# Early loads and sums in an autocorrelation stage, stored operand sums, product order and the engine of a bias add

## The chip, the core and the metric

The kernel runs on one core of a Trainium2 chip. A core has a tensor engine (PE) for matrix products, VectorE (DVE), ScalarE (ACT) and GpSimd (POOL) for elementwise work, and SyncE (SP), whose queue issues the DMA transfers here. Each engine works through its own instructions in order. The metric is the device time of one execution in microseconds (us); several runs are given by their median. The kernel before takes 3541.73 us, the median of 3 runs (3533.64 to 3542.67).

## What is computed

The input `x` has 8 batches of 256 rows and 1024 columns, `ctx` likewise. Four blocks follow each other, each added to `x` with a gate, each on a layer norm of `x`:

```python
x = x + tanh(g_xattn[0]) * autocorrelation(norm(x), ctx, ctx)        # 8 heads, top 11 lags
x = x + tanh(g_ffn[0])   * lora_ffn(norm(x), W, b, A, B, gate_w, gate_b)
x = x + tanh(g_xattn[1]) * attention(norm(x), ctx, ctx, mask, wq, wk, wv, wo)
x = x + tanh(g_ffn[1])   * fourier_ffn(norm(x), W_base, b_base, enc0, enc1, coefs0, coefs1, ...)
...
# autocorrelation
qf, kf = fft(q, axis=2), fft(k, axis=2)
corr = ifft(qf * conj(kf), axis=2).real
w, idx = top_k(corr, 11); w = softmax(w)
out = sum_i w_i * v[min(idx_i + pos, L - 1)]
...
# fourier_ffn: base = x @ W_base.T + b_base; update = irfft of a low-rank product, scaled by 0.5
```

Attention has 32 query heads and 8 key and value heads of 128 columns, with rotary positions. All is in float32.

## The kernel before, in words

The batches go through in two passes (the loop at L1075) of four batches: eight tiles `xt` of 128 rows and 1024 columns stay in SBUF for the whole pass. A pass runs four stages one after the other: autocorrelation with the keys and values of attention beside it, `lora_ffn`, `attention`, `fourier_ffn`.

**Products by sevens.** Every large matrix product is cut into 2 x 2 blocks and done with seven block products instead of eight (Strassen's scheme in Winograd's form). Four of the seven operands of each side are sums: `left_operands` (L175) and `right_operands` (L184) make them with four instructions each. The products run in the order of the tuple `SEVEN` (L37), and `combine` (L192) or `add_product` (L224) spreads each over the result's quadrants:

```python
SEVEN = (1, 2, 6, 7, 5, 3, 4)
```

In `combine`, product 2 finishes quadrant (0,0), 5 finishes (1,1), 3 finishes (0,1) and 4 finishes (1,0). For 5, ACT copies the product and POOL adds it to `u` and to `w`; 3 then needs that `u`. In `add_product`, 7 makes `w` on DVE, and POOL adds it to two parts of `x` (L238, L239); 5 and 4 then add to those parts.

**Autocorrelation.** The Fourier transforms are matrix products with constant cosine and sine matrices. `turn` (L407) works on a half batch: one batch and 512 of its 1024 columns, so eight turns a pass and one more to end. It loads `cn`, `end` and `xr` (the context's two halves, one row of it, and the reversed second half of `x`), normalizes the two parts of `x` on ACT (`xn`, L424), and makes sums and differences on POOL: `ke`, `ko` from the context, `qe`, `qo` from `xn` (L428 to L431). `dft` (L377) transforms these; `products` (L391) multiplies spectra on DVE and adds on POOL (`re`, `im`); `correlation` transforms back, and `lags` (L520) finds the eleven largest lags on DVE and their softmax weights `w`. The sums of those, `both` (L505, L506), are the input of the second half of the work, which is done for the half batch `before` in the next turn: transposes (L468), spectra, products, and back with L483. Between these steps `fill(n)` takes the next pieces of `keys_values` (L653): the products for keys `ps_k` and values `ps_v` (L726), whose weights' sums are in pass 0 made on POOL (L142, L146), after the first weight's. The tile framework may place an instruction of one engine earlier or later than the text has it; the order in the engine's queue is then fixed.

SBUF tiles of 4 KB per partition come from rings of seven buffers, one for each group "a", "b" and "xn" (`big_tile`, L100). `xn`, the product tiles `ma` and `mb`, `w` and `both` share the group "xn".

**The last layer's weight.** `fold_last_layer` (L248), at the end of pass 0's autocorrelation, adds the low-rank Fourier update to `W_base`, so that the last feed-forward is one product. For each of eight tiles of 128 rows it loads a part of the weight (`w1in`, L283), two matmuls with 40 rows make the update (`acc`, L286; two PSUM buffers), DVE adds it (L293), and the sum is stored in DRAM as `w1_d` (L294).

**The feed-forwards.** Both work by pairs of row tiles. `ffn_weight` (L164) loads the four quadrants of the weight (eight loads of 512 KB by the class `Halves`) and returns a function that makes the four sums on DVE: eight instructions of 128x1024 at L128 (class `Both`). `lora_ffn` (L551) and `fourier_ffn` (L1016) call it in each pass, after the first pair's left operands. A pair is normalized (`xn`, L312), transposed on PE (L322), its left operands `s` are made (L178 to L181; on DVE for the first pair, on POOL after it), and seven products (L612 and L1053) are added to `x`. `fourier_ffn` adds its bias to each row tile on POOL in `prepare` (L1037). `lora_ffn` also multiplies by `ag` (L568), chooses a rank by DVE instructions, and multiplies by `bl`.

**Attention.** Sixteen steps a pass (two blocks of 512 rows, eight groups of heads). A step's queries are made in the step before (`ps_q`, L851; rotary in `rope`, L642, whose last add is on POOL, L651), `scores` (L891) is softmax of one batch n and one pair of heads, `values` (L928) applies the weights, and `outputs` (L864) multiplies with `wo` in the step after. In the first block of pass 0 the weights' sums are made on DVE and stored; later steps load all seven operands. `load_wq` and `load_wo` issue these loads on SP.

Of the kernel before, what the change touches and what calls it, by code (L numbers as in the profile page):

```python
# [18 lines left out]
P = 128  # L19
# [17 lines left out]
SEVEN = (1, 2, 6, 7, 5, 3, 4)  # L37
# [7 lines left out]
def flamingo_kernel(ctx: ExitStack, tc: tile.TileContext, a: dict, out: bass.AP):  # L45
# [39 lines left out]
    w1_d = dram.tile([2, 2, P, KH, HALF], F32, name="w1_d")  # L85
# [17 lines left out]
    class Halves:  # L103
# [5 lines left out]
        def load(self, src):  # L109
            for i, t in enumerate(self.t):  # L110
                nc.sync.dma_start(t, src[:, i * KQ : (i + 1) * KQ, :])

# [51 lines left out]
    def ffn_weight(eng, groups, src):  # L164
# [8 lines left out]
        return lambda: right_operands(Both(eng), q, t1, t2, t4)  # L173
# [74 lines left out]
    def fold_last_layer(group, pools):  # L248
# [32 lines left out]
        for c in range(KC):  # L281
            wt = big_tile(group, [2, HALF], "w1in")
            nc.sync.dma_start(wt, a["w1"][c * P : (c + 1) * P, :])  # L283
            for h in range(2):
                acc = ps_kv.tile([P, HALF], F32, tag="kv", name="acc")
                nc.tensor.matmul(  # L286
                    acc,
                    encr[:, c * P : (c + 1) * P],
                    dec[:, h * HALF : (h + 1) * HALF],
                    start=True,  # L290
                    stop=True,
                )
                nc.vector.tensor_add(wt[:, h, :], wt[:, h, :], acc)  # L293
            nc.sync.dma_start(w1_d[c // KH, :, :, c % KH, :].rearrange("h p d -> p h d"), wt)  # L294
            yield
# [39 lines left out]
    def autocorrelation(p, xt, pools, beside):  # L335
# [68 lines left out]

        def turn(this, before):  # L407

            if this:
                b, h = this  # L410
                cols = slice(h * HALF, (h + 1) * HALF)
                r0 = (p * BP + b) * S
                cn = w1.tile([P, 2, HALF], F32, tag="cn", name="cn")
                nc.sync.dma_start(
                    cn, a["ctx"][r0 : r0 + S, cols].rearrange("(s p) d -> p s d", p=P)
                )

                end = w1.tile([P, HALF], F32, tag="end", name="end")
                nc.sync.dma_start(end, a["ctx"][r0 + P, cols].partition_broadcast(P))
                xr = w1.tile([P, HALF], F32, tag="xr", name="xr")  # L420
                nc.sync.dma_start(xr, a["xr"][r0 // 2 : r0 // 2 + P, cols])
                xn = big_tile("xn", [2, HALF], "xn")
# [120 lines left out]
        for b in range(BP):  # L543
            for h in range(2):
                before = turn((b, h), before)
                if b == 0 and h == 0:
                    normalize(1, BP)
# [696 lines left out]
```

## Time and profile before

| what | value |
|---|---|
| median of 3 runs | 3541.73 us (3533.64 to 3542.67) |
| the profiled execution | 3532.26 us, its span 3530.3 us |
| PE busy | 3402.2 us, 96% of the span |
| DVE, POOL, ACT busy | 2203.3, 1460.3, 860.9 us |
| mean granted clock of PE | 0.980 |
| DMA | 418.86 MB, mean 119 GB/s |

The span runs from the first to the last instruction of the profiled execution. A busy share is that of all stages together. In the waits view a line names the instruction that waited and what released it, with the total, the number and the longest of these waits. In a timeline a line gives start, length, engine, source line, operation, output and inputs with shapes, how many of these in a row, and in brackets the engine's idle time before it with what ended it. The granted clock is the share of full speed that PE was given.

The stages of pass 0 lie, by the timeline, at about 0 to 422 us (autocorrelation, keys and values), 422 to 608 (the fold and the first feed-forward), 608 to 1681 (attention) and 1681 to 1799 (second feed-forward); those of pass 1 follow in the same way, up to 3530.

### The profile page before, as it was taken

How to read it: one execution, taken by the hardware profiler on the slowest of the kernel's cores; microseconds unless marked ns; L12 is line 12 of the kernel's file. 1: busy time of each engine (PE TensorE's matmuls, PEld its weight loads, DVE VectorE, ACT ScalarE, POOL GpSimd, SP SyncE). 2: the span in 40 equal slices, each digit the busy share in tenths (PEclk: the TensorE clock that was granted, in tenths of full speed). 3: DMA queues.
4: the chain of work that ended last, by engine and by line, in shares of the span. 5: the costliest groups of instructions: out<-in, count | busy, mean ns of one | idle time of the engine just before them, and what ended most of it. 6: DMA issues, size and time to landing. Idle time of an engine off the chain costs nothing. (4 is left out here: it accounts for less than half of the span.)

```text
span 3530.3 us, 37030 instructions
## 1 busy us (share of the span) xinstructions
PE 3402.2 (96%) x12888; PEld 2310.2 (65%) x12888; DVE 2203.3 (62%) x4141; ACT 860.9 (24%) x2065; POOL 1460.3 (41%) x1275
## 2 busy tenths in 40 slices
PE   7899999899999999999899999999999999999999
PEld 5666645776776776765456666567776776776644
DVE  7667456777777665666557575456566666566662
ACT  2222101222222322222122321113232322222220
POOL 4654212344443344345645542223344344344454
PEclk9999989999999999999999999999999999999999
DMA  6342523334333333333153433043333333333311
GB/s 231 128 151 92 178 98 109 124 132 146 128 133 127 117 123 124 117 125 102 48 200 104 147 99 126 1 155 100 124 117 123 114 122 121 121 116 123 113 39 48
DMA packets 158759, 418.86 MB, mean 119 GB/s; under 512 B 21060, under 2 KB 56132, under 8 KB 158574
## 3 DMA queue, kind: packets, MB, share of 16 engines
q1 hardware_dynamic: 158574, 416.51, 35.3%
q8 instruction: 102, 1.67, 0.2%
q14 instruction: 83, 0.68, 0.1%
HBM read 345.15 MB, written 71.30 MB: 118 GB/s over the span
## 5 line engine op out<-in xcount | busy, mean ns | idle before, releaser
L651 POOL TENSOR_TENSOR qT<-rope,rope 128x512 f32<-128x512 f32 x128 | 167.0, 1305 | 794.3 <-DVE rope L650 794.3
L880 PE MATMUL po<-wo,oT 128*128 128x512 f32 x960 | 432.4, 593 | 0.0
L851 PE MATMUL ps_q<-xn,wq 128*128 128x256 f32 x1920 | 431.5, 380 | 0.0
L851 PEld LDWEIGHTS ps_q<-xn,wq 128*128 128x128 f32 x1920 | 366.6, 191 | 51.3 <-PE po L621 0.5
L327 DVE SCALAR_TENSOR_TENSOR x<-po,tg,x 128x512 f32<-128x512 f32 x360 | 258.5, 742 | 196.9 <-POOL x L230 51.9
L913 ACT ACTIVATE s<-s,nmx 128x256 f32<-128x256 f32 x512 | 255.9, 500 | 299.0 <-DVE nmx L910 298.8
L908 DVE COPY_PREDICATED s<-keep,ps_s 128x512 f32<-128x512 uint8 x256 | 185.7, 728 | 220.4 <-PE ps_s L899 220.0
L880 PE MATMUL po<-wo,oS 128*128 128x512 f32 x640 | 287.4, 596 | 4.4 <-DVE c L220 4.4
L880 PEld LDWEIGHTS po<-wo,oT 128*128 128x128 f32 x960 | 175.8, 190 | 175.6 <-issue 165.2
L851 PE MATMUL ps_q<-xn_t,wq 128*128 128x256 f32 x1280 | 289.3, 379 | 0.0
L940 ACT COPY wT<-pt 128x512 f32<-128x512 f32 x256 | 137.9, 588 | 602.9 <-PE pt L934 602.9
L851 PEld LDWEIGHTS ps_q<-xn_t,wq 128*128 128x128 f32 x1280 | 243.2, 190 | 33.1
L899 PE MATMUL ps_s<-kT,qT 128*128 128x256 f32 x1024 | 251.0, 382 | 11.5 <-POOL qT L651 11.5
L945 PE MATMUL av<-wT,v 128*128 128x256 f32 x1024 | 246.0, 383 | 3.1 <-ACT wT L940 3.1
L945 PEld LDWEIGHTS av<-wT,v 128*128 128x128 f32 x1024 | 191.4, 190 | 77.8 <-issue 43.5
L648 DVE TENSOR_TENSOR rope<-c,tab 128x512 f32<-128x512 f32 x160 | 124.8, 780 | 162.5 <-POOL c L212 139.6
L922 DVE TENSOR_SCALAR s<-s,tot 128x256 f32<-128x256 f32 x512 | 220.4, 471 | 6.7
L907 POOL MEMSET s<- 128x512 f32 x256 | 129.4, 530 | 223.2 <-PE pt L934 221.6
L899 PEld LDWEIGHTS ps_s<-kT,qT 128*128 128x128 f32 x1024 | 192.3, 191 | 38.9 <-POOL qT L651 13.1
L880 PEld LDWEIGHTS po<-wo,oS 128*128 128x128 f32 x640 | 121.4, 191 | 146.0 <-issue 133.5
L910 DVE TENSOR_REDUCE nmx<-s 128x2 f32<-128x512 f32 x256 | 175.0, 685 | 8.3
L235 POOL TENSOR_TENSOR x<-x,part 128x512 f32<-128x512 f32 x80 | 105.0, 1314 | 152.6 <-DVE part L327 143.5
(260 smaller groups left out, 5755.3 us busy)
## 6 DMA issues: line engine op xcount, KB each, us to landing
wq<-in_wq_dram SPq DMA_DIRECT2D x104, 512.0 KB, 3.3
wo<-in_wo_dram SPq DMA_DIRECT2D x104, 512.0 KB, 3.3
wq<-wq_d SPq DMA_DIRECT2D x96, 512.0 KB, 3.3
wo<-wo_d SPq DMA_DIRECT2D x96, 512.0 KB, 3.3
wk<-in_wk_dram SPq DMA_DIRECT2D x26, 512.0 KB, 4.7
wv<-in_wv_dram SPq DMA_DIRECT2D x26, 512.0 KB, 3.9
wk<-wk_d SPq DMA_DIRECT2D x24, 512.0 KB, 4.3
wv<-wv_d SPq DMA_DIRECT2D x24, 512.0 KB, 3.3
```

Source lines behind the costliest of these rows:

```text
L327: nc.vector.scalar_tensor_tensor(xs, ps, g, xs, ALU.mult, ALU.add)
L651: nc.gpsimd.tensor_add(dst, t0, t1)
L851: nc.tensor.matmul(ps[:, l, :], wops[r][:, l, c, :], xo[r][:, c, :], start=(c == 0), stop=(c == KH - 1),)
L880: nc.tensor.matmul(po, ops[r][:, h, t * P : (t + 1) * P], wops[r][:, h, :], start=(h == 0), stop=(h == 1),)
L899: nc.tensor.matmul(ps[:, t, :], qT[i, n][:, l, t * P : (t + 1) * P], kT[:, n * S : (n + 1) * S], start=True, stop=True,)
L907: nc.gpsimd.memset(s, MASKED)
L908: nc.vector.copy_predicated(s, keep[b], ps)
L910: nc.vector.tensor_reduce(nmx, s, AX.X, ALU.max, negate=True)
L913: nc.scalar.activation(s[:, t, :], s[:, t, :], AF.Exp, bias=nmx[:, t : t + 1], accum_out=tot[:, t : t + 1],)
L922: nc.vector.tensor_scalar(s[:, t, :], s[:, t, :], tot[:, t : t + 1], None, ALU.mult)
L940: nc.scalar.copy(wT[i], pt)
L945: nc.tensor.matmul(av[:, i, :], kv[step][1][:, n * 2 + c, :], wT[i][:, c, :], start=(c == 0), stop=(c == 1),)
```

## The change

Four things change.

1. In autocorrelation, `turn` is cut up. `loads` issues the three loads of a half batch, `sums` does its normalization and its sums. A turn issues the loads of the next half batch at its start and makes its sums after the second `fill(2)`, ahead of the work for the half batch before. `end` has two buffers for that. `left` and `took`, the scratch tiles of `lags`, go from two buffers to one.
2. The feed-forward weights' sums are made once. `lora_ffn`'s are stored in DRAM in pass 0 (`w0_d`) and loaded in pass 1. `fold_last_layer` now works in four rounds on two row tiles each, makes the four sums of the last layer there on DVE and stores all seven operands (`w1_d`); `fourier_ffn` loads them in both passes (`stored_weight`: fourteen loads of 512 KB).
3. The order of the seven products is 1, 2, 6, 7, 4, 5, 3, everywhere; loads of stored operands follow it.
4. `fourier_ffn` adds its bias on DVE, at the start of a pair's `project`, instead of on POOL in `prepare`.

```diff
-SEVEN = (1, 2, 6, 7, 5, 3, 4)
+SEVEN = (1, 2, 6, 7, 4, 5, 3)
+WEIGHTS = (1, 2, 3, 5, 6, 4, 7)
...
-    w1_d = dram.tile([2, 2, P, KH, HALF], F32, name="w1_d")
+    w0_d, w1_d = (dram.tile([7, P, KH, HALF], F32, name=f"w{i}_d") for i in range(2))
...
+        def store(self, dst):
+            for i, t in enumerate(self.t):
+                nc.sync.dma_start(dst[:, i * KQ : (i + 1) * KQ, :], t)
...
-        return lambda: right_operands(Both(eng), q, t1, t2, t4)
+        def make():
+            ops = right_operands(Both(eng), q, t1, t2, t4)
+            for i, r in enumerate(WEIGHTS):
+                if r > 3:
+                    ops[r].store(w0_d[i])
+            return ops
+        return make
+
+    def stored_weight(groups, where):
+        ops = {}
+        for n, r in enumerate(SEVEN):
+            ops[r] = Halves([groups[(2 * n + i) // 7] for i in range(2)], f"w_{r}")
+            ops[r].load(where(r))
+        return ops
...
-        for c in range(KC):
-            wt = big_tile(group, [2, HALF], "w1in")
-            nc.sync.dma_start(wt, a["w1"][c * P : (c + 1) * P, :])
...
-                nc.vector.tensor_add(wt[:, h, :], wt[:, h, :], acc)
-            nc.sync.dma_start(w1_d[c // KH, :, :, c % KH, :].rearrange("h p d -> p h d"), wt)
+        for c in range(KH):
+            wt = []
+            for k in range(2):
+                rows = slice((k * KH + c) * P, (k * KH + c + 1) * P)
+                wt.append(big_tile(group, [2, HALF], "w1in"))
+                nc.sync.dma_start(wt[k], a["w1"][rows, :])
+            for k in range(2):
...
+                    nc.vector.tensor_add(wt[k][:, h, :], wt[k][:, h, :], acc)
+                if k == 0:
+                    yield
+            q = [[wt[k][:, j, :] for j in range(2)] for k in range(2)]
+            t12, t47 = big_tile(group, [2, HALF], "w_t12"), big_tile(group, [2, HALF], "w_t47")
+            nc.sync.dma_start(w1_d[0, :, c, :], q[0][0])
+            nc.vector.tensor_sub(t12[:, 0, :], q[0][1], q[0][0])
+            nc.vector.tensor_sub(t47[:, 1, :], q[1][1], q[0][1])
+            nc.vector.tensor_sub(t12[:, 1, :], q[1][1], t12[:, 0, :])
+            nc.vector.tensor_sub(t47[:, 0, :], t12[:, 1, :], q[1][0])
+            for i, t in ((1, wt[1]), (3, t12), (5, t47)):
+                nc.sync.dma_start(w1_d[i : i + 2, :, c, :].rearrange("r p d -> p r d"), t)
             yield
...
-        def turn(this, before):
+        def loads(this):
+            b, h = this
+            cols = slice(h * HALF, (h + 1) * HALF)
+            r0 = (p * BP + b) * S
+            cn = w1.tile([P, 2, HALF], F32, tag="cn", name="cn")
...
+            end = w1.tile([P, HALF], F32, tag="end", name="end", bufs=2)
...
+            xr = w1.tile([P, HALF], F32, tag="xr", name="xr")
...
+            return b, cols, cn, end, xr
+
+        def sums(b, cols, cn, end, xr):
+            xn = big_tile("xn", [2, HALF], "xn")
...
+            nc.gpsimd.tensor_add(ke, cn[:, 0, :], cn[:, 1, :])
+            nc.gpsimd.tensor_sub(ko, cn[:, 0, :], cn[:, 1, :])
+            nc.gpsimd.tensor_add(qe, xn[:, 0, :], xn[:, 1, :])
+            nc.gpsimd.tensor_sub(qo, xn[:, 0, :], xn[:, 1, :])
+            nc.vector.scalar_tensor_tensor(ke, end, -2.0, ke, ALU.mult, ALU.add)
+            return b, cols, end, qe, qo, ke, ko
+
+        def turn(this, before, coming):
+            after = None
             if this:
...
+                b, cols, end, qe, qo, ke, ko = this
+                if coming:
+                    coming = loads(coming)
                 kr_ps, ki_ps = dft(CE, ke), dft(SE, ko)
...
+                if coming:
+                    after = sums(*coming)
                 fill(2)
...
-            left = w2.tile([P, S], F32, tag="left", name="left")
-            took = w2.tile([P, S], F32, tag="took", name="took")
+            left = w2.tile([P, S], F32, tag="left", name="left", bufs=1)
+            took = w2.tile([P, S], F32, tag="took", name="took", bufs=1)
...
-            make_w = ffn_weight(nc.vector, groups, lambda k, j: w1_d[k, j])
+            w = stored_weight(groups, lambda r: w1_d[WEIGHTS.index(r)])
...
-                nc.gpsimd.tensor_add(xt[t], xt[t], bias1)
                 return xnT
...
+                for i in range(2):
+                    nc.vector.tensor_add(xt[m * 2 + i], xt[m * 2 + i], bias1)
                 for r in SEVEN:
...
-        make_w0 = ffn_weight(nc.vector, (gb, ga), lambda k, j: a["w0"][k, j])
+        if p == 0:
+            w0, make_w0 = {}, ffn_weight(nc.vector, (gb, ga), lambda k, j: a["w0"][k, j])
+        else:
+            made = {1: a["w0"][0, 0], 2: a["w0"][1, 0], 3: a["w0"][1, 1]}
+            w0 = stored_weight((gb, ga), lambda r: made.get(r, w0_d[WEIGHTS.index(r)]))
+            make_w0 = None
```

## The prediction

> **What bounds the kernel now.** I read the page first, then the waits of the tensor engine (PE), then timelines at the places which those waits name. Page, part 2, in 40 slices of 88 us:
>
> ```profile
> span 3530.3 us, 37030 instructions
> ...
> PE 3402.2 (96%) x12888; PEld 2310.2 (65%) x12888; DVE 2203.3 (62%) x4141; ACT 860.9 (24%) x2065; POOL 1460.3 (41%) x1275
> ...
> PEclk9999989999999999999999999999999999999999
> ```
>
> PE is busy for 96% of the span. It is idle for only 3530.3 - 3402.2 = 128 us, and its mean granted clock is 0.980. A half clock throughout 4% of the span (141 us) gives such a mean, so up to 70 us more is hidden in matmuls that run at half speed. The change adds no matmul and removes none; whatever it gains must come out of these two parts. The list of PE's waits (who waited for whom, total us, times, longest) says where:
>
> ```profile
> PE dft L379 <- POOL qe L430: 44.4, 14, 11.0
> PE ps_s L899 <- POOL qT L651: 11.5, 4, 4.9
> PE po L1053 <- DVE s L180: 11.1, 2, 6.6
> ...
> PE pt L322 <- DVE xa L583: 5.1, 1, 5.1
> ...
> PE po L880 <- DVE c L220: 4.4, 2, 2.2
> ```
>
> A gap costs more than its length. The windows view over stretches after such gaps (length, PE busy, the other engines, granted clock, DMA share, GB/s):
>
> ```profile
> 445.50:476.30 30.80, 29.66 (x56) 13.44 (x55) 15.56 (x37) 1.41 (x4) 0.00 (x0) 0.50 0.59 202
> ...
> 2063.00:2070.00 7.00, 5.88 (x10) 3.23 (x11) 4.96 (x6) 0.00 (x0) 5.26 (x5) 0.53 0.29 106
> ```
>
> The second follows a gap of 3.04 us: 5.9 us of PE work are done at half clock, which loses another 2.9 us. So each gap below is counted as its length plus half of the PE work in the half-clock stretch behind it. The first row is the folding of the last layer's weight: PE is never idle for long there, yet has half clock for 31 us.
>
> **Part 1, autocorrelation: next half batch summed during this one.** The timeline at the start of one turn of pass 1:
>
> ```profile
> 2059.24 0.80 ACT L424 ACTIVATE xn<-x,lin 128x512 f32<-128x512 f32 x1
> 2059.41 1.27 POOL L505 TENSOR_TENSOR both<-w 128x512 f32<-128x512 f32 x1 [9.93 <-ACT w L540]
> ...
> 2062.36 1.71 POOL L430 TENSOR_TENSOR qe<-xn 128x512 f32<-128x512 f32 x1
> ...
> 2064.12 2.07 PE L379 MATMUL dft<-qe,mats 128*128 128x512 f32 x2 [3.04 <-POOL qe L430]
> ```
>
> The normalized input and the sum `qe` stand on ScalarE (ACT) and GpSimd (POOL) behind the last weights `w` and the two `both` of the turn before; PE waits 3.04 us. In the changed kernel's built order `qe` and `qo` stand half a turn earlier on POOL, directly behind `re` and `im` of the running turn. They are then done some 20 us before PE asks. The 44.4 us of waits go, with one exception. In turn 1 of pass 0 (5.6 us) PE's order soon comes to `ps_k` products that need a weight's second sum, which POOL finished at 78.9; PE without its wait on `qe` would be there near 74: the wait changes its name, and I count nothing. Left: 38.8 us. Half-clock work behind the gaps, from the windows: 3.8 + 5.9 + 5.6 + 4.7 + 5.9 + 5.5 = 31.4 us, half of it 15.7. Sum 54.5. What is late next? `both` is done at 2062.4 and its first transpose runs at 2077.6; `im` ends at 2071.7 and is first read at 2088.8. Slacks of 15 and 17 us bear a gain of 3 us per turn. `left` and `took` with one buffer each undo the pairing of two lag searches on VectorE (DVE): a pair now takes 3.9 us, two chains after one another 2 x 2.5 = 5.0; 2.2 us more DVE work per turn, inside those slacks. The loads move up half a turn on the SP queue; `xr` and `cn` there wait for ACT's and POOL's reading of the last ones, which is done by then. POOL gets no new work here. I take nine tenths, **-49 us**; ends -20 (another wait comes up in each turn) and -60 (the 5.6 us too).
>
> **Part 2, product order 1,2,6,7,4,5,3.** `scores` of batch n=0 needs quadrants (0,0) and (1,0). Quadrant (1,0) comes from product 4, until now the last of seven; as the fifth it is ready two products (2 x 3.44 us) earlier, which covers the longest wait, 4.9. Waits 11.5, half-clock work behind them 5.0 and 3.0, so 4.0: 15.5 at most. Now product 3 is last and needs POOL's `u+m`; but 5 stood straight ahead of 3 before too. In `add_product` product 4 now follows 7 and needs POOL's `x+w`; 5 stood there before and needed the later of the same two adds. **-12 us**; ends 0 and -16.
>
> **Part 3, stored sums in place of DVE sums.** Each sum is a DVE instruction 128x1024 of 1.22 us (L128), eight per layer and pass. Where they hurt is DVE's queue. In the attention's last step they wait for their loads, with the evacuation `c` (L220) behind them: waits 4.4, and half clock for 3.4 us of PE work behind each, 3.4: 7.8. **-6 us**, ends 0 and -8. At pass 1's first feed-forward, eight of them stand ahead of `x` L327 (PE gap 2.88) and of `xn` (gap 5.09), with 9 us of half-clock work behind (4.5): 12.5. But `ag`, which the next matmuls read, is issued last on SP, behind the stores of `v` and now 14 loads instead of 8: before at 2194.0, the matmul at 2199.7. That wait takes the sums' place. **-5 us**, ends 0 and -12.
>
> The extra traffic: 8 stores of w0, 7 MB of w1 sums instead of 4, and 3 x 6 more loads of 512 KB. In the fold four loads issued together landed 1.7 us apart, so 18 loads cost 31 us of DMA time; they lie in attention's last steps (DMA share 0.4) with 35 us of outputs of older steps to run first. Without that cover wo's loads, which stand behind them on SP, would be late by up to 10 us a pass. The w0 stores wait on SP for the DVE sums at about 490; behind them stand attention's first loads, wanted at 607, while DMA carries 1 GB/s. Nothing for both.
>
> **Part 4, bias from POOL to DVE.** The timeline of pass 0's second feed-forward:
>
> ```profile
> 1686.04 16.59 POOL L1037 TENSOR_TENSOR x<-x,bias 128x1024 f32<-128x1024 f32 x6
> ...
> 1692.10 2.83 DVE L178 TENSOR_TENSOR s<-xnT 128x512 f32<-128x512 f32 x1
> ...
> 1700.35 2.82 DVE L180 TENSOR_TENSOR s<-s,xnT 128x512 f32<-128x512 f32 x1
> ...
> 1703.23 1.22 PE L1053 MATMUL po<-w_t,s 128*128 128x512 f32 x1 [6.60 <-DVE s L180]
> ```
>
> L178 took 0.68 us at 455.9 with POOL idle, and 2.83 here: beside POOL's long adds each DVE instruction lasts as long as one of those. As DVE instructions the adds cost 1.22. In the built order DVE does, from 1685 on: three normalizations (0.8 each), two biases, three sums of 0.68, some 7 us, plus waiting for PE's transposes: s4's predecessor `s2` is done near 1694, and PE finishes products 1 and 2 at 1696.6. The waits (11.1) and the half-clock work (5.8 and 6.1, so 6.0) go: 17. Sixteen adds a pass cost DVE 20 us, while it is busy 12.5 of 50 us in that stage. **-15 us**, ends -8 and -18.
>
> **Part 5, the fold makes all seven operands (pass 0, once).** Before: eight single tiles between 436.5 (first load issued) and 472.5 (first product of the feed-forward), 36 us. After: four rounds of two loads, adds, four DVE sums, four stores, then the next two loads behind those stores on SP. Seven buffers, less `encr` and `dec`, leave five, and a round takes four. One round: first landing 4.0, second +1.7, two adds 1.4, three sums behind the last add 2.1, four issues 1.6: 10.8 us. Three rounds and the start of the fourth make 38: +2. That is with PE never in the way. Here a rule of the Trainium skill must be weighed ("TensorE: Matmul & The Clock Gate", Part 1): the clock is halved after an idle window of about 3.4 us and returns after about 3.4 us of sustained work. By it a PE as busy as here (29.7 of 30.8 us) would have its full clock, a pair of L286 matmuls would take 1.7 us, and the loss stays near +4. The row above shows 0.50 in spite of that, and a pair takes 3.6 us (x8 records, four matmuls, 7.2 us). With two accumulators, the second pair of a round can start only when the first pair is evacuated, so 3.6 us go on top of each round: 4 x 3.6 = 14.4. The trace decides: +16. Behind it the loads of w0's last quarter (ga's tiles) are as late as the fold, and product 6 needs them through two sums; products 1 and 2 and the next transposes (12.5 us) cover that as before. I take **+14 us**; ends +2 and +24.
>
> **Sum.** -49 - 12 - 6 - 5 - 15 + 14 = -73 us. The profiled execution took 3532.3 us (span 3530.3 and 2.0 around it): 3459. The median of the three runs is 3541.7, two of them at 3542 and one at 3533.6; from the median it is 3469. I say **3463 us**, that is -73 from 3536, between the two.
>
> **Rivals.** (a) *The next wait takes over in autocorrelation.* DVE is busy 33 of 47 us in the turn at 2061; if lag searches and products now collide there, only the 20 us end is left, and the fold costs 24: -20-12-6-5-15+24 = -34, about 3502. Against it: the slacks of 15 us. (b) *The fold hides and everything goes*: -60-15-8-10-17+4 = -106, about 3430. For it: PE order puts feed-forward transposes between the fold's pairs; against: the same was so before at half clock. (c) *Slower: the ring of seven "xn" tiles fills up.* `xn` now lives through the middle of a turn beside `both`, four product tiles and the new `w`: seven of seven, where six were the most before. If a product tile has to wait for a release in every turn, DVE stops with the lag searches behind it, and `both` comes late. All else gains 24 us (12+6+5+15-14), so it decides from a wait of more than 24/16 = 1.5 us a turn on top of losing part 1 whole; at 5 us a turn it gives 3536 - 24 + 80 = 3592. Against it: the product tiles are released within 9 us, `w` is first written 15 us later. (d) *It doesn't do what it says*: POOL still reaches `qe` late, since everything there keeps one queue; then -24, 3512.
>
> **How the numbers follow.** The sum's case, all parts about as sized: 0.62, range 3435 to 3492. (a) 0.17, (b) 0.10, (d) 0.06, (c) 0.05. Low end 3425, beyond (b); high end 3510, which takes in (a) and leaves out (c) and most of (d). A measurement of this kernel can't tell 0.3% (11 us) from no change; the first four cases are all faster by more, except for the tail of (d). Faster 0.92, same 0.03, slower 0.05.
>
> **What would show it.** Right: no PE wait on `qe` beyond the first turns; no wait of L1053's matmul on `s`; the sums s at 0.7 us there; scores' wait on `qT` under 4 us in all; the first feed-forward's products starting about 14 us later than the fold's start would have given before. Wrong: a row of waits on `both`, `re` or `ps_v`'s evacuation of 1 us or more in each turn; the half clock persisting beyond 500 us in pass 0; outputs waiting for wo.

## The result, and the profile after

The changed kernel takes 3475.86 us (median of 4 runs, 3473.84 to 3476.34). The kernel before took 3537.68 us on the same chip (3533.02 to 3542.67). The ratio is 0.9824, with a 95% interval of 0.9806 to 0.9842: 1.8% faster, 62 us. The prediction was 3463 us, 73 us faster, with a range of 3425 to 3510.

The page of the changed kernel, its parts 1 and 2 (in the row of clocks a digit is tenths of full speed in one of 40 slices of 87 us):

```profile
span 3471.7 us, 37174 instructions
...
PE 3372.3 (97%) x12888; PEld 2303.4 (66%) x12888; DVE 2209.5 (64%) x4149; ACT 860.4 (25%) x2065; POOL 1412.9 (41%) x1259
...
PEclk8999979999999999999999999999999999999999
```

PE's idle time fell from 128.1 us to 3471.7 - 3372.3 = 99.4. Of the span's 58.6 us, 28.7 are idle time and 29.9 are matmuls that took less time. Over the stretches with half clock in each trace, PE was busy 120.4 us before and 76.2 after; half of the 44.2 between them, 22.1 us, is what the clock gave back, and some 8 us of PE's busy time I can't assign. The slice with a 7 (434 to 521 us) holds the fold. PE's list of waits (who waited for whom: total us, times, longest):

```profile
PE acc L313 <- DVE w1in L320: 15.1, 3, 6.3
PE px L637 <- DVE xa L635: 12.0, 7, 1.8
PE ps_k L774 <- POOL wk_s L152: 9.4, 1, 9.4
PE pt L359 <- DVE xn L349: 8.7, 2, 5.2
PE pa L616 <- DMA ag<-in_ag_dram: 6.8, 1, 6.8
...
PE ps_v L774 <- DVE v L238: 5.5, 1, 5.5
...
PE ps_v L774 <- DVE c L238: 3.3, 1, 3.3
```

The 44.4 us of waits on `qe`, the 11.5 on `qT` and the 11.1 on `s` are gone from the list. In their place stand waits in the fold (`w1in`) and one on `wk_s`, and the seven on `xa` have grown to 12.0 us. Before:

```profile
PE px L589 <- DVE xa L587: 4.4, 7, 0.8
```

A sum by waits does not tell where the time went, so I cut the profiled execution of each kernel where PE begins a stage and compared the lengths. This table is the base of all that follows (us). In pass 0 the first feed-forward's row begins with its first product, since the fold runs ahead of it. A wait of PE just ahead of a feed-forward's first transposes counts as part of that feed-forward.

| stage | before, pass 0 | after, pass 0 | before, pass 1 | after, pass 1 |
|---|---|---|---|---|
| autocorrelation, keys and values | 421.5 | 412.1 | 392.8 | 363.6 |
| fold, to the first product | 51.0 | 63.7 | - | - |
| (rest of the) first feed-forward | 135.1 | 138.7 | 148.4 | 153.6 |
| attention | 1073.1 | 1059.8 | 1067.5 | 1056.1 |
| last feed-forward | 119.3 | 111.1 | 117.2 | 108.6 |

The differences are -9.4, +12.7, +3.6, -13.3, -8.2 in pass 0 and -29.2, +5.2, -11.4, -8.6 in pass 1, in sum -58.6. Two of them, +3.6 and +5.2, the prediction did not have: both first feed-forwards got longer. The first stage of pass 0 varies by itself: in seven profiled executions whose code there is the changed kernel's it took 407.3 to 412.5 us, 409.3 in the mean. Of the other stages, the fold takes 63.7 to 66.9 us where its code is the same and pass 0's last feed-forward 109.9 to 112.4; the rest repeat more closely, attention of pass 1 within 0.1.

The last feed-forward of pass 0 in the changed kernel, timeline (start, length, engine, line, operation, output and inputs):

```profile
1685.97 0.68 DVE L200 TENSOR_TENSOR s<-xnT 128x512 f32<-128x512 f32 x1
...
1687.90 0.68 DVE L202 TENSOR_TENSOR s<-s,xnT 128x512 f32<-128x512 f32 x1
...
1689.83 1.21 DVE L1097 TENSOR_TENSOR x<-x,bias 128x1024 f32<-128x1024 f32 x1
```

The sums `s` take 0.68 us where they took 2.83, and the last of the two that product 6 needs is done at 1688.6, before PE gets there. The bias costs 1.21 us on DVE, as estimated from L128's 1.22.

### The profile page after: what moved, and what is told of

Read it like the earlier page. It is cut to its first block, busy times and chain, and to the rows that moved or that the text cites. A ratio compares the mean times of both kernels' runs of the same rounds, so it can differ in the third digit from the quotient of the medians.

```text
span 3471.7 us, 37174 instructions
## 1 busy us (share of the span) xinstructions
PE 3372.3 (97%) x12888; PEld 2303.4 (66%) x12888; DVE 2209.5 (64%) x4149; ACT 860.4 (25%) x2065; POOL 1412.9 (41%) x1259
## 5 line engine op out<-in xcount | busy, mean ns | idle before, releaser
L252 POOL TENSOR_TENSOR x<-x,part 128x512 f32<-128x512 f32 x80 | 115.0, 1437 | 255.1 <-ACT part L251 255.1
L696 DVE TENSOR_TENSOR rope<-c,tab 128x512 f32<-128x512 f32 x160 | 116.4, 728 | 154.0 <-POOL c L234 147.3
```

## Experiments

All ratios are against the kernel before on the same chip. The changed kernel's is 0.9824; 0.001 is 3.5 us, and intervals are 0.0013 to 0.0016 to each side, so that a step of less than 5 us is read from the stages and not from the ratio.

### The old product order

```diff
-SEVEN = (1, 2, 6, 7, 4, 5, 3)
+SEVEN = (1, 2, 6, 7, 5, 3, 4)
```

> The changed kernel with the old product order 1,2,6,7,5,3,4 everywhere. Theory (the order gives what attention gained and costs something in the first feed-forward): attention's two stages, which went from 1073.1 and 1067.5 to 1059.8 and 1056.1 us, lose some 9 us each again; the waits of px on xa, 1.8 us each in the changed kernel, fall back to 0.5 to 0.8, which gives 8 us; the waits of ps_v on c and v in pass 0's autocorrelation shrink by 5. In all +5 us, about 3481 (3474 to 3490). Rival (px and ps_v have nothing to do with the order): they stay, and the time rises by 18, about 3494. Second rival (attention's gain was the stored sums', not the order's): scores' waits on qT stay short, and the time falls by about 10, to 3466.

Measured: 3480.02 us, ratio 0.9849 (0.9834 to 0.9863): 9 us slower than the changed kernel. Attention takes 1068.8 and 1064.8 us, 9.0 and 8.7 more. The rest goes the other way: the first feed-forwards take 135.3 and 150.2 us, 3.4 less each, the last ones 108.1 and 106.9, 3.0 and 1.7 less. The list of waits:

```profile
PE ps_s L947 <- POOL qT L699: 12.0, 4, 5.5
...
PE pt L359 <- DVE xn L349: 5.5, 2, 2.8
...
PE px L637 <- DVE xa L635: 5.2, 7, 1.2
```

The waits on `qT` are back with 12.0 us; those on `xa` fell from 12.0 to 5.2, and those on `xn`, at the start of the last feed-forwards, from 8.7 to 5.5. So the new order gave 17.7 us in attention, cost 6.8 in the first feed-forwards and up to 4.7 in the last ones, where the 3.0 is hardly more than that stage varies by. In keys and values the theory failed. The waits on `v` and `c` did not shrink by 5 us; they grew from 8.8 to 16.6. The stages with autocorrelation took 415.1 and 366.2 us, longer than the 407.3 to 412.5 of the changed kernel's code and than its 363.6, so there the new order gave something too; how much is open, since this profiled execution, of 3486.22 us, was the longest of four.

Why `px` waits is to be seen in the two timelines. Before, with PE's work between `pa`, whose result the rank is chosen from, and `px`:

```profile
506.45 1.07 PE L626 MATMUL po<-bl,xaT 65*128 65x512 f32 x2
...
507.37 1.04 PE L322 MATMUL pt<-ident,xn 128*128 128x128 f32 x8
...
508.24 2.74 PE L612 MATMUL po<-w,xnT 128*128 128x512 f32 x6
...
511.55 0.32 PE L589 MATMUL px<-ident,xa 128*65 128x128 f32 x1 [0.57 <-DVE xa L587]
```

After:

```profile
502.30 2.79 PE L660 MATMUL po<-w_t,s 128*128 128x512 f32 x6
...
506.88 0.29 PE L637 MATMUL px<-ident,xa 128*65 128x128 f32 x1 [1.80 <-DVE xa L635]
```

DVE's chain of small instructions from `pa` to `xa` takes 4.9 us before (506.65 to 511.50) and 4.2 after (502.50 to 506.74). Before, PE had 1.07 + 1.04 + 2.74 us of other work in that time, with small overlaps; after, it has 2.79. In the queue of the new order the transposes and the part of a product no longer stand in this place.

### The order in parts

The new order only in queries and in keys and values; `outputs` and both feed-forwards, with the loads of their weights, by a second tuple:

```diff
+OUT = (1, 2, 6, 7, 5, 3, 4)
...
-                for r in SEVEN:
+                for r in OUT:
```

> The changed kernel with the new product order only in queries and in keys and values; outputs and both feed-forwards go back to 1,2,6,7,5,3,4. Theory (from the stages of the run with the old order everywhere: it lost 17.7 us in attention through scores' waits on qT, and gained 3.4 us in each first feed-forward and 3.0 and 1.7 in the last ones): scores keep their short waits, px on xa falls from 12 to about 5 us in all, and the time falls by 11, to about 3465 (3461 to 3469). Rival (attention's gain needs the order in outputs too, whose additions stand in the same DVE queue as the queries' evacuations): attention loses 9 us a pass again, and the time rises by 7.

Measured: 3463.33 us, ratio 0.9806 (0.9793 to 0.9820), 6 us below the changed kernel's ratio. Attention keeps 1061.3 and 1056.1 us, the waits on `xa` are down to 5.2 us, and the first feed-forwards take 135.3 and 150.0. So the gain in attention is the queries' alone, and the first feed-forwards' loss is their own order's. The last ones (110.4, 108.5) didn't get the 3.0 and 1.7 us back: that part of the expectation failed, and what the old order gave there stays open.

### Autocorrelation as before

`turn` loads and sums its own half batch again, and `left` and `took` have two buffers. These three are undone together; no run takes them apart. The core of it:

```diff
-                if coming:
-                    coming = loads(coming)
...
-                if coming:
-                    after = sums(*coming)
...
+                nc.gpsimd.tensor_add(qe, xn[:, 0, :], xn[:, 1, :])
+                nc.gpsimd.tensor_sub(qo, xn[:, 0, :], xn[:, 1, :])
```

> The changed kernel with autocorrelation as before (a turn loads and sums its own half batch; left and took with two buffers). Theory: part 1 gave what the two autocorrelation stages gained, 9 us in pass 0 and 29 us in pass 1; undone, the time is 3476 + 38 = 3514 (3505 to 3522), and the waits on qe are back with some 40 us. In pass 0 the waits on wk_s, on c and on v fall back from 18 to about 3 us if they come from the moved sums. Rival (those waits in pass 0 come from the product order): they stay, and with qe's waits on top the time is near 3525.

Measured: 3501.77 us, ratio 0.9913 (0.9896 to 0.9929): 31 us slower than the changed kernel, not 38. The stages: 385.9 us in pass 1, 22.3 more than the changed kernel; 415.5 in pass 0, 6.2 above the mean of 409.3. The wait is back:

```profile
PE dft L416 <- POOL qe L465: 35.8, 14, 5.0
```

It is 35.8 us, not 44.4: with the new order two of these waits are shorter than they were before (the one near 111 us has 3.8 us instead of 11.0, the one in pass 1's third turn 1.5 instead of 4.8). The remaining 6.9 us of pass 1 (392.8 to 385.9) therefore go to the other changes. Of these the product order is the only one that touches this stage's body, yet undone by itself it lost only 2.6 us there (366.2 against 363.6), so the other 4.3 are gain that either part alone would have brought.

In pass 0 the waits on `qe` here come to 20.6 us, and the early sums returned only some 6. The waits on POOL's `wk_s`, on `c` and on `v`, 18.2 us in the changed kernel, are down to 1.8 (on `v`). So these come from the moved sums and not from the product order, as the theory had it.

### Pass 0: who holds the second turn up

In the changed kernel the second turn of pass 0 looks like this:

```profile
76.09 1.26 POOL L465 TENSOR_TENSOR qe<-xn 128x512 f32<-128x512 f32 x1
...
77.31 1.71 POOL L148 TENSOR_TENSOR wk_s<-wk,wk 128x512 f32<-128x512 f32 x1
78.98 1.71 POOL L440 TENSOR_TENSOR im<-mb,ma 128x512 f32<-128x512 f32 x1
...
82.32 2.47 POOL L152 TENSOR_TENSOR wk<-wk,wk 128x512 f32<-128x512 f32 x2
84.76 2.48 POOL L152 TENSOR_TENSOR wk_s<-wk_s,wk 128x512 f32<-128x512 f32 x2
86.07 3.78 PE L774 MATMUL ps_k<-cx_t,wk_s 128*128 128x256 f32 x8 [9.36 <-POOL wk_s L152]
```

POOL works without a pause from 76.09 on, and PE waits 9.4 us for the sums of the second key weight. That is the turn whose old wait of 5.6 us on `qe` the prediction had counted at nothing. I moved these sums to DVE:

```diff
-                ops = left_operands(Short(nc.gpsimd), w, *s)
+                ops = left_operands(nc.vector if kind == "wk" else Short(nc.gpsimd), w, *s)
```

> The changed kernel with the sums of the second key weight in pass 0 made on DVE (four adds of 128x1024, 1.22 us each) instead of on POOL (eight of 128x512). Theory (in pass 0 part 1 gave 6 to 9 us and not 28, because POOL's queue, relieved of nothing, now has the next turn's qe ahead of these sums: the wait of ps_k on wk_s of 9.4 us with 10 us at half clock behind it is the old wait on qe under a new name): that wait falls under 2 us and the first stage, 407 to 412 us in the runs of this code, takes 9 to 13 us less. Rival (the sums wait for their weight's loads, not for POOL): the wait keeps 6 us or more, on DVE, and the stage gets at most 3 us shorter, or longer where DVE's lag searches are held up.

Measured: 3472.64 us, ratio 0.9826 (0.9813 to 0.9839): no change. The first stage takes 408.8 us. The wait on `wk_s` is gone, and another has come:

```profile
72.46 2.24 POOL L436 TENSOR_TENSOR re<-ma,mb 128x512 f32<-128x512 f32 x1
...
74.66 3.98 POOL L465 TENSOR_TENSOR qe<-xn 128x512 f32<-128x512 f32 x1
...
78.60 2.24 POOL L466 TENSOR_TENSOR qo<-xn 128x512 f32<-128x512 f32 x1
...
80.81 1.71 POOL L440 TENSOR_TENSOR im<-mb,ma 128x512 f32<-128x512 f32 x1
...
82.56 1.22 PE L564 MATMUL ps_cor<-inv,im 128*128 128x256 f32 x2 [7.11 <-POOL im L440]
```

Now `im` stands behind the next turn's `qe` and `qo`, which take 3.98 and 2.24 us instead of 1.26. Both sides of the expectation failed: the named wait went, and the stage got no shorter.

### The bias on POOL again

```diff
                 transposed(xnT, xn, ps_t, "t")
+                nc.gpsimd.tensor_add(xt[t], xt[t], bias1)
                 return xnT
...
-                for i in range(2):
-                    nc.vector.tensor_add(xt[m * 2 + i], xt[m * 2 + i], bias1)
```

> The changed kernel with the bias added by POOL in prepare, as before. Theory: the second feed-forward, which went from 118.4 and 117.1 us to 110.3 and 108.7, takes 8 us more a pass again: 3476 + 16 = 3492 (3486 to 3496); the waits of its products on s are back with 10 us or more in all. Rival (the sums that no longer stand in DVE's queue made that gain): the time stays within 5 us of 3476.

Measured: 3479.94 us, ratio 0.9847 (0.9833 to 0.9862). The last feed-forwards take 114.2 and 111.9 us, 3.1 and 3.3 more, not 8 each. In the timeline of pass 0's last feed-forward the long additions and what they do to DVE are back, but little of the wait:

```profile
1680.87 11.21 POOL L1083 TENSOR_TENSOR x<-x,bias 128x1024 f32<-128x1024 f32 x4 [0.63 <-DVE xn L349]
...
1687.04 2.83 DVE L200 TENSOR_TENSOR s<-xnT 128x512 f32<-128x512 f32 x1
...
1692.55 0.68 DVE L202 TENSOR_TENSOR s<-s,xnT 128x512 f32<-128x512 f32 x1
...
1693.28 3.70 PE L1099 MATMUL po<-w,s 128*128 128x512 f32 x8 [1.59 <-DVE s L202]
```

PE waits 1.59 us for `s` where the kernel before waited 6.60: without the weight's sums in its queue DVE comes through in spite of POOL. So the stored sums without the bias take 5.1 and 5.3 us off these stages, with the new order's cost there in the figure.

### The fold and the last layer's sums as before

Eight single tiles, four quadrants stored, and the four sums made on DVE in each pass:

```diff
-            w = stored_weight(groups, lambda r: w1_d[WEIGHTS.index(r)])
+            w = {}
+            make_w = ffn_weight(nc.vector, groups, lambda k, j: w1_d[k, j], False)
```

> The changed kernel with the last layer's fold and its feed-forward's weight as before: eight single tiles, four quadrants stored, four sums made on DVE in each pass. Theory (the bias on DVE alone gave 6.4 of the 16.5 us by which the two last feed-forwards got shorter; the sums that left DVE's queue gave the other 10): the fold is 13 us shorter, the feed-forwards together 10 longer, attention's last step up to 6 longer: in all -3 to +3 us against the changed kernel, near 3476. Rival (the two causes cover each other, so that either alone is enough): the feed-forwards stay within 3 us and the time falls by 10, to 3466.

Measured: 3466.90 us, ratio 0.9813 (0.9800 to 0.9827), 4 us below the changed kernel. The fold takes 52.3 us, 11.4 less. The last feed-forwards take 110.7 and 108.6 us, no more than with stored sums, so the rival was right here: with the bias on DVE the sums cost these stages nothing. Attention takes 1064.7 and 1060.3 us, 4.9 and 4.2 more, through the waits at its end that the prediction named:

```profile
PE po L914 <- DVE c L239: 4.0, 2, 2.0
```

Storing the last layer's sums thus gave 9.1 us, all in attention's last steps, and cost 11.4 in the fold.

### The first feed-forward's sums remade in pass 1

```diff
-        if p == 0:
...
-            w0 = stored_weight((gb, ga), lambda r: made.get(r, w0_d[WEIGHTS.index(r)]))
-            make_w0 = None
+        w0, make_w0 = {}, ffn_weight(nc.vector, (gb, ga), lambda k, j: a["w0"][k, j])
```

> The changed kernel in which pass 1 loads the quadrants of w0 and makes their four sums on DVE again, as before (pass 0 still stores them). Theory (after the first run of the order undone: the stored w0 gave nothing at the start of pass 1's first feed-forward, since ag, and behind it a tile whose place is free only when the last v is stored, hold it as long): the stage after pass 1's autocorrelation stays within 2 us of 153.6, and the time within 3 us of the changed kernel's. Rival (the sums did hold DVE's queue and the stored ones took that away, as in the prediction): that stage is 5 us longer or more, and the time rises by 5.

Measured: 3475.83 us, ratio 0.9836 (0.9823 to 0.9850). The stage takes 151.6 us against 153.6, the one before it 366.3 against 363.6, and the ratio is the same within the intervals. The stored `w0` gave nothing.

### ag and bl ahead of the weights

```diff
-            w0 = stored_weight((gb, ga), lambda r: made.get(r, w0_d[WEIGHTS.index(r)]))
...
                 nc.sync.dma_start(ag, a["ag"])
                 nc.sync.dma_start(bl, a["bl"])
+                if p:
+                    w0 = stored_weight((gb, ga), from_dram)
```

> The changed kernel with ag and bl loaded ahead of the fourteen loads of w0 in pass 1. Theory (ag, last on SP's queue, is what holds the first feed-forward's start in pass 1: a wait of 6.8 us and a half clock of 10 us behind it): that wait goes, and the time falls by 7 to 11 us, to about 3467. Rival (the transfers are late whatever comes first, since their buffers come free late): the wait moves to the first product, which waits for w, and the time stays within 3 us of 3476.

Measured: 3470.90 us, ratio 0.9821 (0.9806 to 0.9836): no change. The stage takes 152.3 us, 1.3 less. What ended the wait is in the timeline:

```profile
2149.96 0.81 DVE L349 TENSOR_SCALAR xn<-x,mv,rstd 128x1024 f32<-128x1024 f32 x1 [3.42 <-DMA v_d<-v]
...
2151.94 3.69 PE L616 MATMUL pa<-ag,xnT 128*128 128x68 f32 x16 [4.25 <-ACT xnT L360]
```

The 6.8 us on `ag` became 4.25 on `xnT`, and that one goes back to the second `xn`, which DVE could write only when the last `v` had been stored (landed at 2149.9). The start of this stage is held by two things that end within 2.5 us of each other.

### The fold with early loads

The two sum tiles of a round in the ring "xn", and a round's loads issued ahead of the stores of the round before:

```diff
-        for c in range(KH):
+        def w1_loads(c):
...
+        coming = w1_loads(0)
+        for c in range(KH):
+            wt = coming
+            if c + 1 < KH:
+                coming = w1_loads(c + 1)
...
-            t12, t47 = big_tile(group, [2, HALF], "w_t12"), big_tile(group, [2, HALF], "w_t47")
+            t12, t47 = big_tile("xn", [2, HALF], "w_t12"), big_tile("xn", [2, HALF], "w_t47")
```

In the changed kernel a round looks like this: the two loads are issued on SP (SPq) when the stores of the last round have been, and PE and DVE stand idle until they land.

```profile
451.44 1.90 SPq L308 DMA_DIRECT2D w1in<-in_w_dram  x2
457.06 1.28 DVE L320 TENSOR_TENSOR w1in<-w1in,acc 128x512 f32<-128x512 f32 x2 [6.11 <-DMA w1in<-in_w_dram]
...
457.81 4.63 PE L313 MATMUL acc<-dec,encr 40*128 40x512 f32 x5 [5.62 <-DVE w1in L320]
```

> The changed kernel with the fold's two sum tiles in the ring xn, and each round's two loads issued ahead of the stores of the round before. Theory (a round waits for its loads, which stand on SP behind the stores of the last round: gaps of 3.2, 5.6 and 6.3 us): those gaps go, the fold takes 50 instead of 64 us, and the time falls by 11 to 15, to about 3463. Rival (two accumulators, and matmuls of 40 rows at half clock, set the pace of a round by themselves): the gaps go, but a round still takes 7 to 8 us of matmuls with evacuations between; the fold takes 58 us and the time falls by 6 or less.

Measured: 3466.66 us, ratio 0.9812 (0.9799 to 0.9825), 4 us below the changed kernel's. The fold takes 53.2 us, 10.5 less, but the rest of the feed-forward takes 145.9, 7.2 more:

```profile
PE po L667 <- DVE w_t L134: 3.8, 1, 3.8
PE acc L320 <- DVE w1in L327: 3.5, 2, 2.4
```

The wait on `w1in` fell from 15.1 to 3.5 us, and product 6 of the feed-forward now waits 3.8 us for `w0`'s sums, with half clock behind it. This is the cover of 12.5 us that the prediction had found for w0's last loads: with a shorter fold it is used up.

### What helps, together

Split order, early loads of the fold, `ag` first, and the key weight's sums on DVE in one kernel:

> The changed kernel with four edits together: the split order, the fold's sums in the ring xn with early loads, ag and bl ahead of w0, and the second key weight's sums on DVE. If what each gave alone adds up (order 10, fold 4 to 9, ag 1, key weight's sums 9 to 13): 3476 - 24 to - 33, that is 3443 to 3452. Rival (the first stage's gain doesn't come, and the fold's is lost on w0's late loads): 3459 to 3465.

Measured: 3454.98 us, ratio 0.9778 (0.9765 to 0.9792), between the sum of the single gains (3443 to 3452) and the rival (3459 to 3465). The fold takes 49.4 us, the rest of the feed-forward 140.3; the first stage 407.4, which is no gain. The same with the fold's stores issued by POOL:

```diff
-            nc.sync.dma_start(w1_d[0, :, c, :], q[0][0])
+            nc.gpsimd.dma_start(w1_d[0, :, c, :], q[0][0])
...
-                nc.sync.dma_start(w1_d[i : i + 2, :, c, :].rearrange("r p d -> p r d"), t)
+                nc.gpsimd.dma_start(w1_d[i : i + 2, :, c, :].rearrange("r p d -> p r d"), t)
```

> The same four edits, and the fold's stores issued from POOL's queue instead of SP's. Theory (with the fold's loads a round earlier the next wait, 3.8 us for w0's sums with 10 us at half clock behind it, comes from w0's last loads standing on SP behind the fold's last stores): it goes, and the time is 6 to 8 us below that of the four edits alone. Rival (these loads wait for their buffers in the ring, which the last w1in tiles hold until they are stored): within 2 us of the four edits alone.

Measured: 3444.07 us (3442.26 to 3448.92), ratio 0.9749 (0.9736 to 0.9762): 2.5% faster than before, and 0.0075 below the changed kernel's ratio, some 26 us. The wait on `w_t` is down to 0.3 us; the fold takes 43.4 us, less than the 51.0 of the kernel before, though it makes all seven operands. The step from the four edits is 11 us where 6 to 8 were expected. The two last loads of `w0` are issued on SP at 444.6 us instead of 459.3. So SP's queue, not the ring, held them.

### qe and qo on DVE in pass 0

```diff
-            nc.gpsimd.tensor_add(qe, xn[:, 0, :], xn[:, 1, :])
-            nc.gpsimd.tensor_sub(qo, xn[:, 0, :], xn[:, 1, :])
+            eng = nc.vector if p == 0 and b < 2 else nc.gpsimd
+            eng.tensor_add(qe, xn[:, 0, :], xn[:, 1, :])
+            eng.tensor_sub(qo, xn[:, 0, :], xn[:, 1, :])
```

> The version with the fold's stores on POOL's queue, and in addition qe and qo of pass 0's first two batches made on DVE (0.68 us each) instead of on POOL. Theory (what ate the gain in pass 0 is POOL's order at the start of the second turn: with the key weight's sums gone from there, the next turn's qe and qo, one of 4.0 us and one of 2.2 beside DVE's long adds, still stand ahead of im, and ps_cor waits 7.1 us for it): im follows re at once, the wait falls under 2 us and the half clock of 7 to 10 us behind it goes; the first stage falls from 407.0 to about 398, the time from 3444 to about 3435. Rival (the late thing is im's input from DVE, whose queue has the weight's sums and now qe and qo too): the wait stays at 5 us or more, and the time stays within 3 us of 3444.

Measured: 3449.17 us, ratio 0.9758 (0.9745 to 0.9771), the same within the intervals; first stage 409.5. POOL's queue now has `im` straight behind `re`, and still:

```profile
76.11 6.32 POOL L448 TENSOR_TENSOR im<-mb,ma 128x512 f32<-128x512 f32 x1
...
76.62 1.21 DVE L202 TENSOR_TENSOR wk<-wk,wk 128x1024 f32<-128x1024 f32 x1
77.75 1.20 DVE L203 TENSOR_TENSOR wk_s<-wk_s,wk 128x1024 f32<-128x1024 f32 x1
78.89 0.67 DVE L474 TENSOR_TENSOR qe<-xn 128x512 f32<-128x512 f32 x1
79.49 1.20 DVE L204 TENSOR_TENSOR wk_s<-wk,wk_s 128x1024 f32<-128x1024 f32 x1
80.62 0.67 DVE L475 TENSOR_TENSOR qo<-xn 128x512 f32<-128x512 f32 x1
81.23 0.67 DVE L223 TENSOR_TENSOR c<-ps_k,u 128x512 f32<-128x512 f32 x1
...
82.48 1.22 PE L573 MATMUL ps_cor<-inv,im 128*128 128x256 f32 x2 [5.58 <-POOL im L448]
```

`im`, whose other fifteen instances in this run take 1.25 to 2.32 us, takes 6.32 here: it begins at 76.1, and ends 1.1 us after the last of DVE's five additions in a row (81.3). Neither theory named this. POOL's instruction isn't late in its queue, and its inputs were written by 73.2; it stands still while DVE adds. The Trainium skill ("SBUF — State Buffer", in its section on the two separate sides) says that GpSimd shares a pair of ports with a DVE instruction that has two SBUF inputs, as a lock for a whole instruction, so that the other blocks fully. That fits each of the five, and it fits the next DVE instruction, `c`, which has one of its inputs in PSUM and runs while `im` goes on. That a row of five holds POOL out from the first to the last is what this trace adds.

## Why the prediction was right, and where it was not

The time was inside the range, 13 us above the predicted 3463, and the sum of the parts was 73 us where 62 were measured. The mechanisms were right in most parts, but that the sum came so close is partly luck, since errors of both signs met: part 1 was sized some 20 us too high, part 2 by 3 and the stored `w0` by 5, while attention's end, the bias and the fold came out 1 to 3 us better each, and 4 us in pass 1's first stage, which either of two parts would have brought alone, are counted in neither.

*Part 1, -49.* Measured by undoing it: about 29 us by the stages (22.3 and 6.2), 31 by the ratio. The mechanism was right: no wait on `qe` is left, and the 15 us of slack of `both` held in pass 1, which got what the early sums could give. The mis-sized term is pass 0. By the working's own figures the 49 us are 22.5 for pass 1 ((17.0 + 8.05) x 0.9) and 26.5 for pass 0 ((21.8 + 7.65) x 0.9); undoing part 1 cost 22.3 and 6.2. The working took "the wait changes its name, and I count nothing" for one turn, the second, and let the other 21.8 us of waits on `qe` in pass 0 go whole with their half clock. What stood in their place, by the waits after: the second turn's wait grew from 5.6 to 9.4 us, and PE waited 3.3 and 5.5 us for evacuations `c` and `v`, where the kernel before had 3.0 for `v`. The half clock stayed as well: in pass 0's first stage PE was busy 25.4 us at half clock before and 29.6 after, and only its idle time fell, from 48.4 to 38.8 us. In three arrangements of the second turn PE waited 9.4 us for `wk_s`, 7.1 for `im` behind `qe`, and 5.6 for `im` beside DVE's additions, and the stage got no shorter. So by these runs the two elementwise engines together are the limit there, and moving an addition from one to the other moved the wait. Besides, a part of the waits on `qe` was already shortened by the new product order (44.4 to 35.8), so the two parts' gains overlap, and the sum took no account of it.

*Part 2, -12.* In attention it gave 17.7 us, more than the 15.5 that the working called the most; the four waits on `qT` that came back, 12.0, are of the size read before, and the rest lies in half clock and in smaller waits of which I didn't find each. What failed is the step that looked only at `combine` and at DVE's and POOL's side of `add_product`: the feed-forwards' orders were taken as free. They cost 3.4 us twice through `px`, and the last feed-forwards were 3.0 and 1.7 us shorter with the old order everywhere, by a cause left open. Over all the order gave 9 us by the ratios.

*Part 3.* "Attention's end, -6" measured 9.1: right, the step named the wait and its place. "Pass 1's first feed-forward, -5": 0. The working itself had found that "that wait takes the sums' place", and then still took two fifths of the sum. `ag` was in fact last on the queue (issued at 2150.8, its matmul at 2158.5), and with it put first another wait, 2.5 us shorter, took its place. The whole stage grew by 5.2 us, of which 3.4 are the order's. The other 1.8 go with the stored operands: with the sums made again the stage takes 151.6 us, but then the stage before it is as much longer.

*Part 4, -15.* The two stages got 8.2 and 8.6 us shorter, 16.8, with the new order's cost in the figure. But the cause was one of two that each do most of it. The bias on DVE without stored sums gives all of it (110.7 and 108.6 us), the stored sums without the bias 10.4 of 16.8. The prediction gave the stored sums nothing here; as the last of the two changes that is right, as the first it would be wrong. A single undo (+6.4) would have made the bias look worth less than half.

*Part 5, +14.* Measured 12.7 (11.4 by undoing it), by the mechanism described: loads behind the stores on SP, and a second pair of products that waits for the first one's evacuation. From one issue of a round's loads to the next (437.1, 451.4, 464.8) a round took 14.3 and 13.4 us, where the working had 10.8 + 3.6 = 14.4. The weighing of the rule on the clock came out as the row had it. The windows view of the changed kernel's fold (length, PE busy, the other engines, granted clock, DMA share, GB/s):

```profile
440.40:481.40 41.00, 25.15 (x33) 9.08 (x32) 20.88 (x42) 0.56 (x2) 0.00 (x0) 0.50 0.59 207
```

The clock is 0.50 for 41 us here. PE waits in this stretch, so by itself it would not contradict the Trainium skill's page "TensorE: Matmul & The Clock Gate" (Part 1, full clock after about 3.4 us of sustained work); the last section has a stretch that does.

Of the rivals, "the next wait takes over" was the nearest, in pass 0 alone; the ring of seven tiles did not fill: in DVE's list of waits in the changed kernel, `ma` waits only for its inputs (`dft` and ACT's copies `kr`, `kn`, `ki`) and `mb` not at all.

## What to carry to other kernels

When an engine's queue is relieved of one wait, look at what all engines do in that place before counting the gain: if two of them are working without a pause there, the wait can come back under another name whichever instruction is moved, as it did here twice. When two changes take away causes of the same wait, undo each alone and both, since either undo by itself shows too little. And an order that is set in one place for all, such as that of the seven products, is worth splitting by its users: it gained 18 us in attention's queries and lost 7 in the two first feed-forwards.

## What the hardware showed

*A row of DVE additions holds a POOL addition.* 6.32 us for 1.25 to 2.32, beside five DVE instructions in a row (above). The prediction knew the other direction only, where DVE's 0.68 us became 2.83 beside POOL.

*A busy PE had half clock while its matmuls had 40 rows.* The version with the fold's stores on POOL keeps PE nearly always busy in the fold. Windows view, in four stretches:

```profile
426.00:436.00 10.00, 9.45 (x32) 4.04 (x31) 7.96 (x18) 1.17 (x2) 3.43 (x5) 0.99 1.01 338
436.00:450.00 14.00, 12.87 (x14) 3.81 (x14) 9.49 (x17) 0.00 (x0) 5.42 (x8) 0.50 1.00 395
450.00:456.30 6.30, 5.93 (x7) 2.52 (x8) 5.02 (x11) 0.00 (x0) 2.13 (x3) 0.50 1.02 403
456.30:466.00 9.70, 9.09 (x47) 5.80 (x46) 7.11 (x17) 2.17 (x5) 1.26 (x1) 1.00 0.59 240
```

In the first stretch PE is busy 9.45 of 10 us, with the fold's products and transposes between them, and at its end the clock falls to half. In the second it does only those products, 12.87 of 14 us, at half clock; one of them, as the trace counts them, takes 0.91 us (10.95 for twelve) where it took 0.50 in the first stretch (1.98 for four). From 450.4 on it has the feed-forward's products of 128 rows, and 5.9 us later the clock is full. By the Trainium skill's rule of about 3.4 us of sustained work ("TensorE: Matmul & The Clock Gate", Part 1) the clock would not have fallen at 436, and by an estimate from that figure it would have been back near 440; here the measurement decides.

That it is the rows which matter was not tried by itself; a fold with its operands filled up to 128 rows would try it. DMA, the other thing at its full share here, is no likely cause. Its share was 1.01 in the first stretch too, at full clock, and 1.02 in the third, before the clock came back; and the kernel before had half clock in its fold at a share of 0.59.
